# Joining the row scans of layer 1 in a two-layer scanning convolution: two scans per matmul, blocks of rows moved by quarters

## The chip, the core and the metric

One of the eight cores of a Trainium2 chip runs the whole kernel. The metric is device time in microseconds; the time before is 4159.55 us, the median of three runs (4158.39 to 4170.3). TensorE is called PE (its weight loads PEld), VectorE DVE, ScalarE ACT, GpSimd POOL and SyncE SP. SP computes nothing here: it issues transfers.

## The reference

The input x has 32 images of 48 channels, 64 rows and 128 columns, all float32. Each of two layers normalises its input (group norm, 16 groups), runs four scans over it and adds the result to the input. A scan is a recurrence: each line is the input's line plus a one-dimensional convolution (48 channels to 48, five taps along the line) of the line before it.

```python
def step(w, b):
    def f(carry, inp):
        nxt = inp + _conv1d(carry, w, b)
        return (nxt, nxt)
    return f
xs = jnp.moveaxis(x, 2, 0)                                  # rows first
d0 = xs[0]
_, d_rest = jax.lax.scan(step(down_w, down_b), d0, xs[1:])  # down, 63 steps
...
_, u_rest = jax.lax.scan(step(down_w, down_b), u0, seq)     # up, 63 steps, over the rows of D
...                                                         # right and left: 127 steps each over columns
x = x + _L0_conv_ref(_gn(x), ...)
x = x + _L1_conv_ref(_gn(x), ...)
```

The upward scan uses the weights of the downward one.

## The kernel before

The images go in four groups of eight (`GB`). A row of a group is 48 channels x 128 positions x 8 images. Eight neighbouring positions and their channels are put on the partitions (8 x 48 = 384 = `NG` = 3 groups of 128 partitions), and 16 positions x 8 images make `N` = 128 columns. A step of a scan (`step`) is then nine products (`PRODUCTS`): matmuls of a 128 x 128 block of the banded weights with 128 columns of the last line, summed in three PSUM tiles; two of the nine shift by one position and have 120 columns (112 in the column scans). Each product is executed as two instructions, so a step is 18. As soon as a sum is complete, DVE adds it, the bias and the input's line, and writes the new line in place. The nine products are ordered so that the next step starts on sums that are done first.

The work is a list of phases (`PHASES`). A rows phase handles one group of one layer: 63 steps down, then 63 steps up (`scans`, `row_step`). A cols phase handles a pair of groups: 127 steps right, 127 left. Every scan must wait for its own last step, so PE works through them one after another, in the order of the list.

SBUF holds three slots of 32 rows of a group. Phase k keeps rows 0 to 31 and 32 to 63 in the slots that `slots(k)` names; its middle slot is shared with the phase behind it. `row_views` and `row` find a row there. Normalising is done after loading: `scale_rows` on ACT, 24 instructions for a block of rows (each of 3 partition groups by 8 images).

Everything beside the scans stands on an agenda: `at(t, fn, ...)` puts a job before scan step t (a unit is one step), and `catch_up` writes the jobs into the program when the step is reached. So each engine's order, SP's too, is fixed by these numbers, and SP carries out its transfers in that order: one that must wait holds all behind it. `plan_rows` plans loads (`move_rows` in layer 0, `take_rows` in layer 1, which reads layer 0's result), scaling, and the stores of the upward scan's rows by blocks of 8 (`E8`) to the DRAM tensors `upa` and `upb` of the two layers. `plan_cols` plans the loads of the column phases from these, the residual sums and the results (`mid` for layer 0). A position's block of 16 x 8 columns divides into four quarters of 32 (`NQ`, `RUN`), one for each stage of the column scans.

`plan_input` prepares inputs 1 to 3 (groups counted from 0; they are the second to fourth): a piece of four rows per partition is loaded from `in_x` by `take_in` into one buffer `nat`, permuted by POOL (`permute`), stored to `xin` (`put_out`) and summed by ACT for the statistics (`take_others`); six pieces make a group, and `scaling` makes the factors from the sums. `pair_scaling` does so for a pair of groups of layer 1.

The names of the step tiles tell layer, group and direction: `step_12u` is layer 1, group 2, up; `step_10l` is layer 1, pair 0, left.

Of the kernel before, what the change touches and what calls it, by code (L numbers as in the profile page):

```python
# [41 lines left out]
GB = 8  # L42
E8 = 8
# [34 lines left out]
def weight_runs():  # L78
# [40 lines left out]
@with_exitstack  # L119
def kernel(  # L120
# [604 lines left out]
    def row_views(k):  # L725
        return [slot[i].rearrange("p (o h n) -> p o h n", o=NG, h=HALF) for i in slots(k)]

    def row(k, h):
        return row_views(k)[h // HALF][:, :, h % HALF]

    def move_rows(k, h0, h1, to_dram, q=None):

        _, layer, g = PHASES[k]
        view = row_views(k)[h0 // HALF]
        t = (ups if to_dram else source)[layer][g]
        for h in range(h0, h1, E8):
            end = min(h1, h + E8)
            for o in range(NG):
                for e, c0, c1, p0 in pieces(o):
                    here = view[p0 : p0 + c1 - c0, o, h % HALF : h % HALF + end - h]  # L740
# [12 lines left out]

    def take_rows(k, h0, h1, o):

        _, layer, g = PHASES[k]
        view = row_views(k)[h0 // HALF]
        for e, c0, c1, p0 in pieces(o):
            here = view[p0 : p0 + c1 - c0, o, h0 % HALF : h0 % HALF + h1 - h0]
            for q in range(NQ):  # L760
                dma(
                    here[:, :, q * RUN : (q + 1) * RUN],
                    by_quarter(source[layer][g], e, h0, h1, q)[c0:c1],
                )

    def scale_rows(k, h0, h1, groups=range(NG)):
        _, layer, g = PHASES[k]
        scale, offset = coeffs[layer, g]
        view = row_views(k)[h0 // HALF][:, :, h0 % HALF : h0 % HALF + h1 - h0]
        view = view.rearrange("p o h (k b) -> p o b h k", b=GB)  # L770
        for o in groups:
            for b in range(GB):
                args = view[:, o, b], scale[:, o, b : b + 1], offset[:, o, b : b + 1]
                nc.scalar.activation(  # L774
                    args[0], args[0], AF.Identity, bias=args[2], scale=args[1]
                )

    def scale_at_once(k, h0, h1, eng, o0=0, o1=NG):

        _, layer, g = PHASES[k]  # L780
        view = row_views(k)[h0 // HALF][:, o0:o1, h0 % HALF : h0 % HALF + h1 - h0]
        view = view.rearrange("p o h (k b) -> p o (h k) b", b=GB)
        for t, op in zip(coeffs[layer, g], (ALU.mult, ALU.add)):
            t = t[:, o0:o1].unsqueeze(2).to_broadcast([FULL, o1 - o0, (h1 - h0) * NK, GB])
            eng.tensor_tensor(view, view, t, op)
# [131 lines left out]

    def step(key, weights, b_at, src, inp, dst, whole, part):


        ps = [
            ps_step.tile([FULL, N], F32, tag=f"step{o}", name=f"step{o}_{key}")
            for o in range(NG)
        ]
        left = [sum(1 for p in PRODUCTS if p[1] == o) for o in range(NG)]
        seen = [0] * NG
        for i, o, s in PRODUCTS:
            seen[o] += 1
            m = COLUMNS.get((i, o, s), FULL)
            at = FULL * (o - NG * s - i + 1)  # L930
            nc.tensor.matmul(  # L931
                part(whole(ps[o])[0:m], -s),
                weights[:, i, at : at + m],
                part(src(i), s),
                start=seen[o] == 1,
                stop=seen[o] == left[o],
            )
            if seen[o] == left[o]:
                layer, way = b_at
                nc.vector.scalar_tensor_tensor(  # L940
                    dst(o),
                    whole(ps[o]),
                    bd[:, o, layer, way : way + 1],
                    inp(o),
                    ALU.add,
                    ALU.add,
                )

    def row_step(k, h, prev, inp, name):
        _, layer, g = PHASES[k]  # L950

        def part(t, s):
# [8 lines left out]
            lambda o: row(k, h)[:, o],  # L961
            lambda ps: ps,
            part,
        )

    def col_step(k, way, v0, v1):
# [10 lines left out]
        def part(t, s):  # L977
# [9 lines left out]
            col(v1),  # L987
            lambda ps: ps.rearrange("p (m b) -> p m b", b=GB),
            part,
        )  # L990

    def scans(k):
        if PHASES[k][0] == "rows":
            for h in range(1, H):
                yield lambda h=h: row_step(k, h, row(k, h - 1), row(k, h), "d")
            end = last.rearrange("p (o n) -> p o n", o=NG)
            for h in range(H - 2, -1, -1):
                yield lambda h=h: row_step(
                    k, h, row(k, h + 1), row(k, h - 1) if h else end, "u"
                )  # L1000
        else:
            for v in range(1, W):
                yield lambda v=v: col_step(k, RIGHT, v - 1, v)
            for v in range(W - 2, -1, -1):
                yield lambda v=v: col_step(k, LEFT, v + 1, v)

# [16 lines left out]
    def plan_input(g, times, work, lag, nats, perms):  # L1023
# [5 lines left out]
        for j, t in enumerate(times):  # L1029
            nat = nats[j % ahead]  # L1030
            if j == 0 and g > 1:
                at(t - 7, take_in, g, 0, nat)
            for i in range(per):
                perm, r = perms[i % len(perms)], i * rows // per
                at(t + i * work / per, permute, nat, r, perm, [nc.gpsimd])
                at(t + i * work / per + 4, put_out, g, rows * j + r, perm)
            at(t + lag, stats.take_others, pieces_of * j, nat)
            if j + ahead < len(times):
                free = t + 7
                at(free, take_in, g, rows * (j + ahead), nat)  # L1040
        spread(t + work + lag + (0, 2, 32, 5)[g], scaling(f"x{g}", 0, g, stats, (0, 0, 8, 0)[g]), 1)

    def plan_rows(k, t0, prev):
        if k == 1:
            ahead, scaled = (-34, -18, -3, 12), (-12, -2, 17, 33)
        elif prev == "cols":
            ahead, scaled = (-28, -12, 4, 20), (-13, 3, 19, 35)
        else:
            ahead, scaled = (-54, -43, 0, 11), (-22, -8, 16, 30)
        if k:  # L1050
            for i in range(4):
# [11 lines left out]
        if seam:  # L1063
            cuts = cuts[2:]
            end = t0 + 2 * (H - 1)
            at(end - E8, move_rows, k, E8, 2 * E8, True, 0)
# [5 lines left out]
        for h0, h1 in zip(cuts, cuts[1:]):  # L1072
            t = t0 + 2 * (H - 1) - h0
            if k == 0:
                t += 16 if h0 >= HALF else 68
            elif not following:
                t = t0 + 92 + 5 * (H - h1) / E8 + (34 if h1 <= HALF else 0)
            at(t, move_rows, k, h0, h1, True)
        at(
            t0 + H - 1,  # L1080
            nc.gpsimd.tensor_copy,
# [9 lines left out]
    def plan_cols(k, t0, prev):  # L1091
# [5 lines left out]
        for i in range(n):  # L1097
# [92 lines left out]

    starts = [0]
    for kind, *_ in PHASES:
        starts.append(starts[-1] + 2 * ((H if kind == "rows" else W) - 1))
    for k, (kind, layer, _) in enumerate(PHASES):
# [221 lines left out]
    for k in range(len(PHASES)):  # L1416
        for one in scans(k):
            catch_up(done)
            in_order(one)
            done += 1  # L1420
    catch_up(float("inf"))
# [53 lines left out]
```

## Time and profile before

| | |
|---|---|
| time, median of three runs | 4159.55 us |
| time of the profiled execution | 4158.07 us |
| its span | 4156.0 us |
| mean granted clock of TensorE | 0.989 |
| PE busy, PEld busy | 97%, 97% |
| DVE, ACT, POOL busy | 51%, 30%, 20% |
| mean DMA share, bytes | 0.79, 681 MB |
| of these by SP's queue (q1) | 582 MB, 2064256 packets |

The scans lie one behind another from 61.2 us (first step) to 4099.6 us; the last 56 us are the last results. Busy shares are of the span; a PE that is busy is not PE at its peak, since a matmul's end is modelled. Issuing a transfer is not counted as busy time of any engine, so SP's load is read from its queue's own rows (SPq), whose length is the time that the issue took.

### The profile page before, as it was taken

The page shows a single profiled execution, that of the slowest core. Times are in us where ns is not written, and L with a number is a line of the kernel's source. Part 1 is how long each engine was busy: PE and PEld are TensorE (multiplying, and loading weights), DVE is VectorE, ACT ScalarE, POOL GpSimd, SP SyncE. Part 2 cuts the span into 40 slices and gives each one's busy share as a digit, 9 for nine tenths or more (in the row PEclk, how much of TensorE's full clock was granted, in tenths as well). Part 3 has the DMA queues.
Part 4 walks back from the last instruction along what each step waited for, and adds up shares of the span by engine and source line. Part 5 has one row for each costly group of instructions (what it writes and reads, how often), then busy time and mean ns, then how long its engine had stood idle before and what let it go on. Part 6 is the DMA issues. An engine that isn't in the chain of part 4 may idle for free. (4 is left out here: it accounts for less than half of the span.)

```text
span 4156.0 us, 90019 instructions
## 1 busy us (share of the span) xinstructions
PE 4037.8 (97%) x36628; PEld 4019.1 (97%) x36628; DVE 2139.9 (51%) x6496; ACT 1251.1 (30%) x2438; POOL 832.0 (20%) x745
## 2 busy tenths in 40 slices
PE   6999989999999999999999999999999999999994
PEld 5999989999999999999999999999999999999994
DVE  6454444456654454444447665444444444444444
ACT  4645000526974553000007863423000002200122
POOL 5630010424331010010013220000000015610354
PEclk9999999999999999999999999999999999999997
DMA  9887769669979989258519979869289029999799
GB/s 299 221 187 117 126 125 209 211 146 263 206 198 166 165 170 154 44 99 189 116 26 270 183 145 149 141 98 150 49 139 208 1 56 240 301 247 157 152 235 196
DMA packets 2208798, 681.09 MB, mean 164 GB/s; under 512 B 2008976, under 2 KB 2157696, under 8 KB 2183808
## 3 DMA queue, kind: packets, MB, share of 16 engines
q1 hardware_dynamic: 2064256, 582.38, 68.9%
q10 hardware_dynamic: 141568, 87.46, 8.7%
q0 software_dynamic: 2560, 5.51, 0.5%
q8 instruction: 288, 4.72, 0.5%
q14 instruction: 126, 1.03, 0.1%
HBM read 398.32 MB, written 295.14 MB: 167 GB/s over the span
## 5 line engine op out<-in xcount | busy, mean ns | idle before, releaser
L866 POOL TENSOR_TENSOR arena<-arena 128x2048 f32<-128x2048 f32 x80 | 362.8, 4549 | 1479.8 <-PE step_10l L931 466.1
L774 ACT ACTIVATE arena<-arena,offsetr,scaler 128x256 f32<-128x256 f32 x384 | 289.3, 844 | 272.2 <-DMA arena<-mid 220.7
L711 POOL COPY arena<-arena 128x256 f32<-128x256 f32 x340 | 200.8, 651 | 482.2 <-DMA arena<-in_x 453.6
L774 ACT ACTIVATE arena<-arena,offset,scale 128x256 f32<-128x256 f32 (+2 forms) x360 | 249.0, 789 | 148.8 <-DMA arena<-xin 100.7
L931 PE MATMUL step_00r<-arena,early 128*128 128x128 f32 x2286 | 253.3, 274 | 10.5 <-DMA arena<-arena 7.1
L931 PEld LDWEIGHTS step_00r<-arena,early 128*128 128x128 f32 x2286 | 252.4, 186 | 11.4 <-issue 6.1
L650 ACT ACTIVATE early<-arena 128x256 f32<-128x256 f32 x192 | 129.6, 675 | 444.3 <-DMA arena<-xin 308.4
L931 PE MATMUL step_01r<-arena,early 128*128 128x128 f32 x2286 | 251.3, 273 | 7.6 <-DMA arena<-arena 6.2
L931 PEld LDWEIGHTS step_01r<-arena,early 128*128 128x128 f32 x2286 | 250.8, 185 | 8.1 <-issue 6.5
L931 PE MATMUL step_11r<-arena,early 128*128 128x128 f32 x2286 | 249.3, 272 | 0.3 <-DVE arena L940 0.3
L931 PEld LDWEIGHTS step_11r<-arena,early 128*128 128x128 f32 x2286 | 248.7, 184 | 0.8 <-DVE arena L940 0.7
L931 PE MATMUL step_00l<-arena,wleft 128*128 128x128 f32 x2286 | 249.0, 272 | 0.0
L931 PE MATMUL step_10r<-arena,early 128*128 128x128 f32 x2286 | 248.7, 272 | 0.0
L931 PEld LDWEIGHTS step_10r<-arena,early 128*128 128x128 f32 x2286 | 248.5, 184 | 0.2 <-DVE arena L940 0.2
L931 PEld LDWEIGHTS step_00l<-arena,wleft 128*128 128x128 f32 x2286 | 248.6, 184 | 0.0
L931 PE MATMUL step_10l<-arena,wleft 128*128 128x128 f32 x2286 | 248.5, 272 | 0.0
L931 PE MATMUL step_11l<-arena,wleft 128*128 128x128 f32 x2286 | 248.5, 272 | 0.0
L931 PEld LDWEIGHTS step_10l<-arena,wleft 128*128 128x128 f32 x2286 | 248.4, 184 | 0.0
L931 PE MATMUL step_01l<-arena,wleft 128*128 128x128 f32 x2286 | 248.4, 272 | 0.0
L931 PEld LDWEIGHTS step_11l<-arena,wleft 128*128 128x128 f32 x2286 | 248.4, 184 | 0.0
L931 PEld LDWEIGHTS step_01l<-arena,wleft 128*128 128x128 f32 x2286 | 248.4, 184 | 0.0
L298 ACT COPY early<-arena 128x1 f32<-128x1 f32 x2 | 0.4, 192 | 711.3 <-DVE arena L940 711.3
(199 smaller groups left out, 7158.0 us busy)
## 6 DMA issues: line engine op xcount, KB each, us to landing
xin<-arena SPq DMA_DIRECT2D x94, 512.0 KB, 4.1
arena<-in_x SPq DMA_DIRECT2D x18, 2048.0 KB, 11.0
arena<-xin SPq DMA_DIRECT2D x96, 384.0 KB, 9.9
arena<-mid SPq DMA_DIRECT2D x384, 96.0 KB, 3.1
upb<-arena SPq DMA_DIRECT2D x192, 192.0 KB, 3.9
arena<-upb SPq DMA_DIRECT2D x96, 384.0 KB, 12.6
arena<-xin SPq DMA_DIRECT2D x174, 192.0 KB, 4.4
mid<-arena SPq DMA_DIRECT2D x32, 1024.0 KB, 11.2
```

The source lines that it names most:

```text
L298: fn(*args)
L650: nc.scalar.activation(junk[:, 0:n], view[:, b], AF.Identity, accum_out=self.sum[:, i, j : j + 1])
L711: copy(dst[:, r, q], src[:, r0 + r, q])
L774: nc.scalar.activation(args[0], args[0], AF.Identity, bias=args[2], scale=args[1])
L866: eng.tensor_tensor(unit, unit, nat, ALU.add)
L931: nc.tensor.matmul(part(whole(ps[o])[0:m], -s), weights[:, i, at : at + m], part(src(i), s), start=seen[o] == 1, stop=seen[o] == left[o],)
```

## The change

The list of phases is reordered: layer 1's four rows phases now lie behind all of layer 0, one after another. The upward scan of group 1 runs together with the downward scan of group 2, and that of group 2 with the downward scan of group 3 (`JOINED`, `two_row_step`): each product takes 256 columns, 128 of either scan, with the columns of both scans interleaved by position (16 x 2 x 8), and DVE adds both lines in one instruction. Steps of the joint scans count two units on the agenda. Since the new group's rows come in while the old group's go out from the other end, the blocks of eight rows lie in turned order in some slots (`place`, `rows_at`). In the joint phases loads go by blocks of 8 rows, 40 transfers each, and stores too, by quarters, so that also a store of a block is 40 transfers. A load is planned 34 units ahead of its first step, the scaling 17 units ahead.

Inputs 2 and 3 are prepared over two phases each, since the rows phase of layer 1 that lay between layer 0's last two rows phases is gone from there; the loads of rows phase (0, 3) and some other jobs move on the agenda.

```diff
 PHASES:
-    ("rows", 1, 0),
     ("rows", 0, 3),
     ("cols", 0, 1),
+    ("rows", 1, 0),
     ("rows", 1, 1),
     ("rows", 1, 2),
     ("rows", 1, 3),
...
+JOINED = (8, 9)
...
+    def place(k, h):
+        first = k
+        while first in JOINED:
+            first -= 1
+        since = k - first
+        turned = (since + 1) // 2 % 2 if h < HALF else since % 2
+        c = h % HALF // E8
+        return HALF // E8 - 1 - c if turned else c
...
 def step(...):
-            ps_step.tile([FULL, N], F32, tag=f"step{o}", name=f"step{o}_{key}")
+            ps_step.tile([FULL, 2 * N], F32, tag=f"step{o}", name=f"step{o}_{key}")
...
-                part(whole(ps[o])[0:m], -s),
+                part(turn(whole(ps[o]))[0:m], -s),
                 weights[:, i, at : at + m],
-                part(src(i), s),
+                part(turn(src(i)), s),
...
+    def beside(a, b):
+        shift = b.offset - a.offset
+        assert a.ap == b.ap and shift > 0
+        return bass.AP(a.tensor, a.offset, [a.ap[0], (shift, 2), *a.ap[1:]])
...
+    def two_row_step(ku, hu, kd, hd):
...
+            lambda i: both(row(ku, hu + 1), row(kd, hd - 1), i),
+            inp,
+            lambda o: both(row(ku, hu), row(kd, hd), o),
+            lambda ps: ps.rearrange("p (c m b) -> p c m b", c=2, b=GB),
+            part,
+            lambda t: t.rearrange("p c m b -> p m c b"),
...
 def scans(k):
+                if k + 1 in JOINED:
+                    yield 2, lambda h=h: two_row_step(k, h, k + 1, H - 1 - h)
...
 def plan_input(...):
-            if j == 0 and g > 1:
-                at(t - 7, take_in, g, 0, nat)
+            if g > 1:
+                at(t - 7, take_in, g, rows * j, nat)
...
-        spread(t + work + lag + (0, 2, 32, 5)[g], scaling(f"x{g}", 0, g, stats, (0, 0, 8, 0)[g]), 1)
+        t += work + lag + (0, 2, 2, 1)[g]
+        spread(t, scaling(f"x{g}", 0, g, stats, (0, 0, 4, 0)[g]), 1)
...
 def plan_rows(k, t0, prev):
+        down, up = (2 if k in JOINED else 1), (2 if k + 1 in JOINED else 1)
+        t_up = t0 + down * (H - 1)
...
+            if not PHASES[k][1]:
+                ahead, scaled = (-33, -22, 0, 11), (-16, -5, 16, 30)
-        if k:
+        if k in JOINED:
+            for i in range(H // E8):
+                h, t = i * E8, t0 + 2 * i * E8
+                for o in range(NG):
+                    at(t - 34 + 2 * o, take_rows, k, h, h + E8, o)
+                at(t - 17, scale_rows, k, h, h + E8)
+        elif k:
...
-            t = t0 + 2 * (H - 1) - h0
+            t = t_up + up * (H - 1 - h0)
...
+            elif up == 2:
+                t += 1
...
-            at(t, move_rows, k, h0, h1, True)
+            for q in range(NQ) if up == 2 else (None,):
+                at(t, move_rows, k, h0, h1, True, q)
...
 plan_cols:
-                early = 30 if after else 46 if k == 2 else 70
+                early = 30 if after else 46 if k == 2 else 58 if k - 1 in JOINED else 70
-            spread(units[-1][0] + 14, pair_scaling(pair, stats, 3 if pair else 8), 1)
+            spread(units[-1][0] + (14 if pair else 70), pair_scaling(pair, stats, 8), 1)
...
-    times = [starts[2] + 60 + 13.5 * j for j in range(6)]
+    times = [starts[1] + 28 + 16 * j for j in range(2)]
+    times += [starts[2] + 60 + 13 * j for j in range(4)]
     plan_input(2, times, 6, 6, nats, tiles[2:4])
-    times = [t + 15 * j for t in (starts[3] + 42, starts[4] + 24) for j in range(3)]
-    plan_input(3, times, 6, 7, nats, tiles[2:4])
+    times = [starts[2] + 116 + 13 * j for j in range(2)]
+    times += [starts[3] + 42 + 13 * j for j in range(4)]
+    plan_input(3, times, 6, 6, nats, tiles[2:4])
...
-    at(starts[7] + 50, more_weights, "right", 1, RIGHT)
-    at(starts[7] + 54, more_weights, "left", 1, LEFT)
+    at(starts[6] + 50, more_weights, "right", 1, RIGHT)
+    at(starts[6] + 54, more_weights, "left", 1, LEFT)
```

PE's order, one step of the downward scan of layer 1's group 2 before (the tile's number tells which of the three sums a product goes to; the last part is the shape of the output):

```order
L931 MATMUL step_12d_23767<-arena,early 128x128
L931 MATMUL step_12d_23769<-arena,early 128x128
L931 MATMUL step_12d_23769<-arena,early 96x120
L931 MATMUL step_12d_23767<-arena,early 96x120
L931 MATMUL step_12d_23767<-arena,early 128x128
L931 MATMUL step_12d_23769<-arena,early 128x128
L931 MATMUL step_12d_23768<-arena,early 128x128
L931 MATMUL step_12d_23768<-arena,early 112x128
L931 MATMUL step_12d_23768<-arena,early 128x128
```

And the first joint step of group 1 up (row 62) and group 2 down (row 1):

```order
L954 MATMUL step_11u62d_22798<-arena,early 128x16x2x8
L954 MATMUL step_11u62d_22800<-arena,early 128x16x2x8
L954 MATMUL step_11u62d_22800<-arena,early 96x15x2x8
L954 MATMUL step_11u62d_22798<-arena,early 96x15x2x8
L954 MATMUL step_11u62d_22798<-arena,early 128x16x2x8
L954 MATMUL step_11u62d_22800<-arena,early 128x16x2x8
L954 MATMUL step_11u62d_22799<-arena,early 128x16x2x8
L954 MATMUL step_11u62d_22799<-arena,early 112x16x2x8
L954 MATMUL step_11u62d_22799<-arena,early 128x16x2x8
```

The nine products stand in the same order, each over twice the columns, and one joint step replaces two such groups of nine.

SP's order where group 1's rows of layer 1 go out (`upb_93`) and group 2's come in (`mid_86`), before: the end of 80 loads and the first stores of 40.

```order
L287 DMA arena<-mid_86 48x16x32 x8
L287 DMA arena<-mid_86 16x16x32 x4
L287 DMA arena<-mid_86 48x16x32 x8
L287 DMA arena<-mid_86 32x16x32 x4
L287 DMA upb_93<-arena 48x32x32 x2
L287 DMA upb_93<-arena 32x32x32
L287 DMA upb_93<-arena 16x32x32
L287 DMA upb_93<-arena 48x32x32 x2
```

The same place now:

```order
L288 DMA upb_93<-arena 48x8x32 x2
L288 DMA upb_93<-arena 16x8x32
L288 DMA upb_93<-arena 48x8x32 x2
L288 DMA upb_93<-arena 32x8x32
L288 DMA arena<-mid_86 16x8x32 x4
L288 DMA arena<-mid_86 48x8x32 x8
L288 DMA arena<-mid_86 16x8x32 x4
L288 DMA arena<-mid_86 48x8x32 x8
L288 DMA arena<-mid_86 32x8x32 x4
L288 DMA arena<-mid_86 48x8x32 x8
L288 DMA arena<-mid_86 32x8x32 x4
L288 DMA upb_93<-arena 48x8x32 x2
```

Loads have 8 rows of 32 columns instead of 16, stores 8 rows of one quarter instead of 32 runs (8 rows by four quarters), and 40 of the one alternate with 40 of the other. From the first store of group 1 to the last load of group 3 SP's queue has 1028 transfers.

SP's order in the third rows phase of layer 0, where input 3 is prepared (`xin_83`), before:

```order
L287 DMA xin_83<-arena 128x4x256 x4
L287 DMA arena<-in_x 128x8x512
L287 DMA arena<-mid_84 48x16x32 x8
L287 DMA arena<-mid_84 32x16x32 x4
L287 DMA arena<-mid_84 16x16x32 x4
```

And now:

```order
L288 DMA xin_83<-arena 128x4x256 x2
L288 DMA arena<-in_x 128x8x512
L288 DMA xin_83<-arena 128x4x256 x4
L288 DMA arena<-in_x 128x8x512
L288 DMA xin_83<-arena 128x4x256 x6
L288 DMA upa_90<-arena 48x32x32 x2
```

The loads of layer 1's group 0 (`mid_84`) are gone from here, and the last two pieces of input 3 follow each other in this phase instead of in the one after the next scan.

More of the change, by code (lines that the diff above doesn't have):

```diff
@@ L737, in move_rows @@
             end = min(h1, h + E8)
+            view = rows_at(k, h, end)
             for o in range(NG):
                 for e, c0, c1, p0 in pieces(o):
-                    here = view[p0 : p0 + c1 - c0, o, h % HALF : h % HALF + end - h]
+                    here = view[p0 : p0 + c1 - c0, o]
                     if to_dram:
@@ L756, in take_rows @@
         _, layer, g = PHASES[k]
-        view = row_views(k)[h0 // HALF]
+        turned = h1 - h0 > E8 and place(k, h0) > place(k, h0 + E8)
+        if turned:
+            for h in range(h0, h1, E8):
+                take_rows(k, h, h + E8, o)
+            return
+        view = rows_at(k, h0, h1)
         for e, c0, c1, p0 in pieces(o):
-            here = view[p0 : p0 + c1 - c0, o, h0 % HALF : h0 % HALF + h1 - h0]
+            here = view[p0 : p0 + c1 - c0, o]
             for q in range(NQ):
@@ L915, in let_result, with step @@
                 dma(in_output(j, half, e)[c0 * NH : c1 * NH], src[at : at + (c1 - c0) * NH])
-    def step(key, weights, b_at, src, inp, dst, whole, part):
+    def step(key, weights, b_at, src, inp, dst, whole, part, turn=lambda t: t):
         ps = [
-            ps_step.tile([FULL, N], F32, tag=f"step{o}", name=f"step{o}_{key}")
+            ps_step.tile([FULL, 2 * N], F32, tag=f"step{o}", name=f"step{o}_{key}")
             for o in range(NG)
@@ L939, in step @@
                 layer, way = b_at
[L940 to L947, printed above, removed]
+                to, sums, term = dst(o), whole(ps[o]), inp(o)
+                todo = [(to, sums, term)]
+                if isinstance(term, tuple):
+                    todo = [(to[:, c], sums[:, c], term[c]) for c in range(len(term))]
+                for to, sums, term in todo:
+                    nc.vector.scalar_tensor_tensor(
+                        to, sums, bd[:, o, layer, way : way + 1], term, ALU.add, ALU.add
+                    )
     def row_step(k, h, prev, inp, name):
@@ L961, in row_step, with lines, both, inp @@
             lambda o: row(k, h)[:, o],
-            lambda ps: ps,
+            lambda ps: ps[:, 0:N],
             part,
+        )
+    def beside(a, b):
+        shift = b.offset - a.offset
+        assert a.ap == b.ap and shift > 0
+        return bass.AP(a.tensor, a.offset, [a.ap[0], (shift, 2), *a.ap[1:]])
+    def lines(t):
+        return t.rearrange("p (m b) -> p m b", b=GB)
+    def two_row_step(ku, hu, kd, hd):
+        _, layer, g = PHASES[ku]
+        first = slots(ku)[0] < slots(kd)[0]
+        def both(u, d, o):
+            u, d = lines(u[:, o]), lines(d[:, o])
+            return beside(*((u, d) if first else (d, u)))
+        def inp(o):
+            if hu:
+                return both(row(ku, hu - 1), row(kd, hd), o)
+            pair = lines(last.rearrange("p (o n) -> p o n", o=NG)[:, o]), lines(row(kd, hd)[:, o])
+            return pair if first else pair[::-1]
+        def part(t, s):
+            return t[:, max(0, s) : NK + min(0, s)]
+        step(
+            f"{layer}{g}u{hu}d{hd}",
+            wt[f"down{layer}"],
+            (layer, DOWN),
+            lambda i: both(row(ku, hu + 1), row(kd, hd - 1), i),
[4 more added lines that the diff above has]
+            lambda t: t.rearrange("p c m b -> p m c b"),
         )
@@ L993, in scans @@
         if PHASES[k][0] == "rows":
-            for h in range(1, H):
-                yield lambda h=h: row_step(k, h, row(k, h - 1), row(k, h), "d")
+            if k not in JOINED:
+                for h in range(1, H):
+                    yield 1, lambda h=h: row_step(k, h, row(k, h - 1), row(k, h), "d")
             end = last.rearrange("p (o n) -> p o n", o=NG)
             for h in range(H - 2, -1, -1):
-                yield lambda h=h: row_step(
-                    k, h, row(k, h + 1), row(k, h - 1) if h else end, "u"
-                )
+                if k + 1 in JOINED:
+                    yield 2, lambda h=h: two_row_step(k, h, k + 1, H - 1 - h)
+                else:
+                    yield 1, lambda h=h: row_step(
+                        k, h, row(k, h + 1), row(k, h - 1) if h else end, "u"
+                    )
         else:
             for v in range(1, W):
-                yield lambda v=v: col_step(k, RIGHT, v - 1, v)
+                yield 1, lambda v=v: col_step(k, RIGHT, v - 1, v)
             for v in range(W - 2, -1, -1):
-                yield lambda v=v: col_step(k, LEFT, v + 1, v)
+                yield 1, lambda v=v: col_step(k, LEFT, v + 1, v)
     agenda = []
@@ L1064, in plan_rows @@
             cuts = cuts[2:]
-            end = t0 + 2 * (H - 1)
+            end = t_up + up * (H - 1)
             at(end - E8, move_rows, k, E8, 2 * E8, True, 0)
@@ L1188, in last_results @@
             store_result(k, 0, i, perm)
-    starts = [0]
-    for kind, *_ in PHASES:
-        starts.append(starts[-1] + 2 * ((H if kind == "rows" else W) - 1))
+    starts, end = [], 0
+    for k, (kind, *_) in enumerate(PHASES):
+        n = (H if kind == "rows" else W) - 1
+        starts.append(end - 2 * n if k in JOINED else end)
+        end = starts[-1] + (2 if k in JOINED else 1) * n + (2 if k + 1 in JOINED else 1) * n
     for k, (kind, layer, _) in enumerate(PHASES):
@@ L1416 @@
     for k in range(len(PHASES)):
-        for one in scans(k):
+        for units, one in scans(k):
             catch_up(done)
             in_order(one)
-            done += 1
+            done += units
     catch_up(float("inf"))
```

24 lines of the change are left out of this document (13 added, 11 removed).

## The prediction

> **What bounds the kernel now.** I read the page first, then the windows by stage, the list of who waited for whom on PE, and last the queue of SP, which issues nearly all transfers.
>
> ```profile
> span 4156.0 us, 90019 instructions
> PE 4037.8 (97%) x36628; PEld 4019.1 (97%) x36628; DVE 2139.9 (51%) x6496; ACT 1251.1 (30%) x2438; POOL 832.0 (20%) x745
> ...
> 2605.00:2730.70 125.70, 125.47 (x1138) 124.97 (x1137) 60.91 (x190) 63.18 (x84) 0.00 (x0) 1.00 0.86 136
> 2730.70:2855.00 124.30, 124.30 (x1135) 124.30 (x1135) 60.37 (x189) 37.21 (x50) 0.50 (x1) 1.00 0.68 109
> 2855.00:2980.00 125.00, 125.00 (x1134) 124.55 (x1134) 60.66 (x190) 2.50 (x4) 0.00 (x0) 1.00 0.54 96
> ```
>
> The last three rows are group 2 of layer 1 down, the same group up, and group 3 down (columns: window, length, PE, PEld, DVE, ACT, POOL busy, granted clock, DMA share, GB/s). PE is busy for all of each window at full clock. Here TensorE is the only bound, and everything else has slack. PE's waits in the whole run are few, and all lie at the start or at the seams from rows to columns:
>
> ```profile
> PE rows L1333 <- POOL arena L711: 19.9, 1, 19.9
> PE step_00d L931 <- DVE arena L785: 9.2, 1, 9.2
> PE step_00r L931 <- DMA arena<-arena: 7.1, 2, 5.8
> PE step_01r L931 <- DMA arena<-arena: 6.2, 1, 6.2
> L931 PE MATMUL step_12u<-arena,early x1134: 266/275/282, 2730.7 to 2855.0; 128*128 128x128 f32 x126, 128*96 128x120 f32 x63
> ```
>
> The last row gives the price of one step of a row scan: 63 steps of 18 instructions from 2730.7 to 2855.0 are 124.4 us with the last instruction, so 1.975 us a step and 0.110 us an instruction.
>
> SP's queue in the same stage (start, length, name, count):
>
> ```profile
> 2497.12 50.52 SPq L287 DMA_DIRECT2D arena<-mid  x80
> 2547.74 39.18 SPq L287 DMA_DIRECT2D upb<-arena  x40
> 2587.01 49.22 SPq L287 DMA_DIRECT2D arena<-mid  x80
> 2636.33 41.10 SPq L287 DMA_DIRECT2D upb<-arena  x40
> 2677.52 48.47 SPq L287 DMA_DIRECT2D arena<-mid  x80
> 2744.29 56.41 SPq L287 DMA_DIRECT2D upb<-arena  x40
> ```
>
> A group's 64 rows come in by 160 loads and go out by 80 stores. SP issues back to back for nearly 230 us from 2497 to 2726. So one group already costs SP about 98 us of loads (48.5 to 50.5 for 80) and 80 us of stores, 178 of the 250 us that its scans last. SP is second in line, and the page's table of engines does not show it.
>
> **The joint scans on PE.** Each of the 126 pairs of steps becomes one step of 18 instructions with 256 columns (240 for the shifted ones). The nearest longer matmul:
>
> ```profile
> 27.83 11.32 PE L1333 MATMUL rows<-arena,wleft 128*128 128x512 f32 x26
> L1333 PE MATMUL rows<-arena,wleft x40: 592/592/1219, 19.9 to 38.6; 128*128 128x512 f32 x40
> ```
>
> 26 of them take 11.32 us, the last lasting 0.592: (11.32 - 0.592) / 25 = 0.429 us for 512 columns, 0.215 for 256. Two single instructions are 0.220. Between these I take 0.216 and, for 240 columns, 0.2025: 14 x 0.216 + 4 x 0.2025 = 3.83 us a joint step against 3.95. That is 0.12 x 126 = 15 us if nothing else holds PE; the ends are 0 (no gain a column) and 18. No row shows a read that jumps between two rows every 8 elements. The nearest are the column scans, which read in pieces of 8 too:
>
> ```profile
> L931 PE MATMUL step_10l<-arena,wleft x2286: 259/275/328, 3353.5 to 3601.7; 128*128 128x128 f32 x128, 128*96 128x112 f32 x63
> L940 DVE SCALAR_TENSOR_TENSOR arena<-step_02d,bd,arena x189: 281/351/353, 1087.5 to 1218.3; 128x128 f32<-128x128 f32 x189
> ```
>
> 248.3 us for 2286 instructions are 0.109 each, no more than in the row scans, so I add nothing. A sum on DVE takes 0.351 us now and at most 0.70 for twice the columns; between a sum and the matmul that reads it stand four products, 8 x 0.216 = 1.7 us, so it stays covered.
>
> **The joint scans on SP.** This term decides. Blocks of 8 rows are now loaded by 40 transfers (before: 16 rows by 40) and stored by 40 (before: 10), since each of ten pieces is cut into four quarters. For groups 2 and 3 in, and 1 and 2 out, that is 640 loads and 640 stores instead of 320 and 160. The same small store exists already, at the seam after group 1 of a pair:
>
> ```profile
> 1908.73 18.01 SPq L287 DMA_DIRECT2D upa<-arena  x33
> L287 SPq DMA_DIRECT2D upa<-arena x33: 428/470/1610, 1908.7 to 1926.3; - x33
> DMA to landing us min/median/max: 1.6/1.8/3.9
> upa<-arena SPq DMA_DIRECT2D x84, 48.0 KB, 2.1
> arena<-mid SPq DMA_DIRECT2D x384, 96.0 KB, 3.1
> ```
>
> 33 of them back to back take 18.01 us, 0.546 each, and 0.512 without the one of 1.61 us. They land in 1.8 us, and by the program's semaphores each waits only for the one issued eight earlier (4 us ago), so landing does not hold them: issuing does. A load of double size costs 48.47 / 80 = 0.606. So halving a transfer's bytes hardly makes its issue cheaper, and I price both small kinds at 0.53, with 0.51 and 0.58 (stores 0.546, loads still 0.606) as ends. Forty cost 21.2 us, a block in and a block out 42.4; the scan needs such a pair every 8 joint steps, 30.6 us. SP falls behind by about 12 us per block.
>
> How far follows from SP's order, shown with the change. Count time from the first joint step. The store of group 1's last block waits for joint step 8, at 31 us. From there SP has no pause: 1028 transfers, blocks out and blocks in by turns, up to the last load of group 3. They end at 31 + 1028 x 0.53 = 576 us. The last third then lands (2.4 us) and is scaled:
>
> ```profile
> L774 ACT ACTIVATE arena<-arena,offset,scale 128x128 f32<-128x128 f32 x40 | 20.7, 610 | 19.8 <-DMA arena<-xin 19.8
> ```
>
> 8 x 20.7 / 40 = 4.1 us. So joint step 56 of the second pair can go on at 582 us. Before, the same rows were reached after 2 x (63 + 55.7) single steps, 469 us. The difference, **113 us**, is stall net of the 15 us that the joint matmuls save: whatever PE saves here only waits longer. The loads have a lead of 34 units (a unit is one step of a single scan), which lasts up to the sixth block of the first pair: its loads end 31 + (5 x 40 + 28) x 0.53 = 152 us, and with 6 us more it misses joint step 40, at 153 us. From there on PE stands at the start of each block, eleven times, 113 + 15 = 128 us in all, or 11 to 12 us each. What is late next: only 8 joint steps, then group 3's upward scan of 124 us, in which SP's 120 remaining stores (64 us) and the first column loads fit. Anything else that slows PE between two such waits only shortens the next one.
>
> [...]
>
> **Inputs 3 and 4 over two phases each.** Input 4 must now be ready one phase earlier: four of its six pieces go through one buffer during the third row phase. Its cycle:
>
> ```profile
> 1179.11 1.27 SPq L287 DMA_DIRECT2D arena<-in_x  x1
> 1212.74 0.37 SPq L287 DMA_DIRECT2D arena<-in_x  x1
> 1238.24 1.26 SPq L287 DMA_DIRECT2D arena<-in_x  x1
> DMA to landing us min/median/max: 8.6/11.0/13.7
> L582 ACT ACTIVATE early<-arena 128x512 f32<-128x512 f32 x144 | 90.8, 631 | 267.7 <-DMA arena<-in_x 263.6
> L574 ACT ACTIVATE early<-arena,neg_x_x 128x512 f32<-128x512 f32 x144 | 104.0, 722 | 4.7
> L574 ACT ACTIVATION_READ_ACCUMULATOR early<-arena,neg_x_x 128x1 f32 x144 | 26.9, 187 | 0.0
> L931 PE MATMUL step_02u<-arena,early x1134: 266/275/377, 1218.1 to 1345.2; 128*128 128x128 f32 x126, 128*96 128x120 f32 x63
> 1480.40 19.75 SPq L287 DMA_DIRECT2D arena<-xin  x19
> 324.00:448.50 124.50, 124.50 (x1137) 124.50 (x1136) 60.63 (x190) 44.66 (x60) 2.36 (x3) 1.00 0.69 106
> ```
>
> The first three pieces' loads are issued 34 and 26 us apart (the line below them is their time to landing). The fourth would be issued near 1264, land 11 us later, and be summed by ACT in 8 x (0.631 + 0.722) + 16 x 0.187, 13.8 us, until about 1289. DVE's part of the scaling stands in its order near step 95 of that phase, the 32nd of the upward scan, at 1218 + 32 x 2.0 = 1282, and DVE works in order: a stall of 0 to 9 us, I take 4. The first 16 rows of the next phase load right behind it (20 us for 20 transfers), in time for its start at 1345. Two pieces of input 3 move into the row phase of the last line, where POOL, which permutes them, is busy for 2 of 124 us. The relaxed pair scaling and the moved weight loads have their cover on POOL and ACT unchanged: nothing.
>
> Against the profiled execution's own 4158.1 (1.5 below the median of 4159.6, to which I predict): 4159.6 + 113 + 4 = **4277 us**.
>
> **Rivals.** *SP keeps up.* An SP issue that stands alone takes less:
>
> ```profile
> L287 SPq DMA_DIRECT2D arena<-upa x120: 302/308/2300, 487.0 to 1998.5; - x120
> ```
>
> At about 0.35 the 1028 end at 391 us, well before 463, nothing stalls, and the 15 us are gained: 4159.6 - 15 + 4 = 4149, faster. It decides below 0.42 a transfer. Against it stand the 33 in a row at 428 or more; for it, only lone issues. Chance 0.09. [...] *Issue is dearer*: the joint stage mixes loads and stores on the 16 DMA engines, as the load rows do at 0.606; 1028 x 0.61 = 627 gives +195 and 4359. Against it, halved bytes; 0.10. *The main case*, 0.76.
>
> **Range and chances.** The main case by its ends 0.51 and 0.58 reaches from 4256 to 4328, and with 0 to 9 us for input 4 and a queue that starts up to 10 us late, 4240 to 4345. I give 4215 to 4345, which leaves out the fast rival and most of the dear one. 0.3% (12 us) is what a measurement here tells from no change: faster 0.09, same 0.05, slower 0.86.
>
> **What would show it.** Right: in the joint stage SP's rows without gaps, about 0.53 us apiece, 40 and 40 in turn; PE and DVE waiting for ACT's scaling or for the loads from mid at every eighth joint step, 8 to 13 us each; joint matmuls 0.216 us apart; the joint stage 90 to 130 us longer than the same 252 single steps were. Wrong: SP rows near 0.4 us with pauses at the stores' waits (then the kernel is faster), or PE stalls elsewhere, above all in the third row phase (input 4) or a joint matmul far above 0.216.

## The result: 2.7% slower, and the profile after

The changed kernel takes 4272.27 us (median of six runs, 4268.5 to 4281.04), the kernel before 4158.87 us (median of six, 4146.94 to 4170.3). The ratio is 1.0273, 95% interval 1.0256 to 1.029. The profiled execution took 4269.46 us, with a span of 4267.5 against 4156.0 before. The head of its page:

```profile
span 4267.5 us, 86313 instructions
PE 4048.6 (95%) x34360; PEld 3950.1 (93%) x34360; DVE 2073.5 (49%) x6124; ACT 1306.7 (31%) x2630; POOL 823.0 (19%) x745
```

2268 matmuls fewer (126 x 18), and yet PE is busy 11 us longer than the 4037.8 before, with 95% of the span instead of 97%.

The windows over the joint stage, of the kernel before (its 252 single steps) and of the kernel after (the 126 joint steps, then the same split at the first stall). Columns: window, length, PE, PEld, DVE, ACT and POOL busy, granted clock, DMA share, GB/s.

```profile
2478.00:2980.40 502.40, 502.17 (x4562) 500.61 (x4561) 248.57 (x794) 149.38 (x205) 4.77 (x14) 1.00 0.73 119
```

```profile
2496.10:2680.20 184.10, 184.10 (x867) 157.87 (x866) 66.79 (x143) 54.62 (x105) 0.50 (x1) 1.00 0.46 73
2680.20:3092.00 411.80, 327.50 (x1404) 273.01 (x1404) 110.21 (x240) 119.81 (x231) 0.51 (x1) 0.87 0.48 77
2496.10:3092.00 595.90, 511.60 (x2270) 430.88 (x2269) 177.00 (x383) 174.44 (x335) 1.01 (x2) 0.91 0.48 76
```

The stage grew from 502.4 to 595.9 us, by 93.5. Its first 48 joint steps run without a gap, 184.1 / 48 = 3.835 us each. The other 78 would need 299.2 us at that pace and took 411.8. Of the 112.6 us lost, 84.3 are idle (411.8 - 327.5), and the remaining 28.3 are matmuls that ran longer: the granted clock is 0.87 over this window. The DMA share *fell*, from 0.73 to 0.48, so the DMA engines are not what is short.

Who waited for whom on PE, after (in total, times, longest):

```profile
PE step_00r L954 <- DMA arena<-arena: 21.8, 1, 21.8
...
PE step_12u62d L954 <- DMA arena<-mid: 11.1, 1, 11.1
PE step_11u14d L954 <- DMA arena<-mid: 9.8, 1, 9.8
...
PE step_12u6d L954 <- DMA upb<-arena: 7.5, 1, 7.5
```

Ten stalls of 7 to 11 us, at the joint steps u14 and u6 of the first pair and u62, u54 and so on to u6 of the second: at the start of each block of 8 rows, from the seventh block on. The step with the stall also runs slower. The second pair's u6, with its stall inside, and the step after it (durations in ns: least, median, most):

```profile
L954 PE MATMUL step_12u6d<-arena,early x18: 379/607/793, 3054.9 to 3068.9; 128*128 128x256 f32 x12, 128*96 128x240 f32 x4, 128*112 128x256 f32 x2
L954 PE MATMUL step_12u5d<-arena,early x18: 366/379/379, 3069.1 to 3072.7; 128*128 128x256 f32 x12, 128*96 128x240 f32 x4, 128*112 128x256 f32 x2
```

One more stall was not there before: 21.8 us at the first column seam, where the kernel before waited 7.1 in two for the same transfers.

SP's queue in the joint stage, the first and last rows of 26 (start, length, name, count):

```profile
2521.96 20.81 SPq L288 DMA_DIRECT2D upb<-arena  x40
2542.81 20.29 SPq L288 DMA_DIRECT2D arena<-mid  x40
2563.20 21.02 SPq L288 DMA_DIRECT2D upb<-arena  x40
2584.27 21.49 SPq L288 DMA_DIRECT2D arena<-mid  x40
...
3021.59 21.03 SPq L288 DMA_DIRECT2D upb<-arena  x40
3042.66 13.96 SPq L288 DMA_DIRECT2D arena<-mid  x28
```

Each row begins where the one above it ends. From 2521.96 to 3056.62 SP issues 1028 transfers, 534.7 us, 0.520 each: 41.6 us for a block out and a block in, where eight joint steps take 30.7.

### The profile page after: what moved, and what is told of

It reads as the page before. It is cut to its first block, busy times and chain, and to the rows that moved or that the text cites. A ratio compares the mean times of both kernels' runs of the same rounds, so it can differ in the third digit from the quotient of the medians.

```text
span 4267.5 us, 86313 instructions
## 1 busy us (share of the span) xinstructions
PE 4048.6 (95%) x34360; PEld 3950.1 (93%) x34360; DVE 2073.5 (49%) x6124; ACT 1306.7 (31%) x2630; POOL 823.0 (19%) x745
## 5 line engine op out<-in xcount | busy, mean ns | idle before, releaser
L797 ACT ACTIVATE arena<-arena,offsetr,scaler 128x128 f32<-128x128 f32 (+1 forms) x576 | 344.4, 685 | 490.6 <-DMA arena<-mid 447.6
L954 PE MATMUL step_00r<-arena,early 128*128 128x128 f32 x2286 | 251.4, 273 | 23.7 <-DMA arena<-arena 21.8
L911 ACT COPY arena<-arena 128x256 f32<-128x256 f32 x172 | 99.7, 655 | 364.3 <-POOL arena L889 245.9
## 6 DMA issues: line engine op xcount, KB each, us to landing
arena<-upb SPq DMA_DIRECT2D x96, 384.0 KB, 11.3
arena<-mid ACTq DMA_DIRECT2D x29, 1024.0 KB, 11.3
```

The lines of the kernel that those rows point to most:

```text
L797: nc.scalar.activation(args[0], args[0], AF.Identity, bias=args[2], scale=args[1])
L911: copy(by_w(perm)[:, a], src[:, a])
L954: nc.tensor.matmul(part(turn(whole(ps[o]))[0:m], -s), weights[:, i, at : at + m], part(turn(src(i)), s), start=seen[o] == 1, stop=seen[o] ...
```

## The experiments

Two theories stood against each other for the joint stage: SP's issue time per transfer, or something that goes with the transfers themselves (bytes, the DMA engines, a load that must wait for the store of its place). For the seam: SP late because of the third input's two pieces (group 2, "input 3" in the expectations), or the DMA engines late. Each edit is against the changed kernel if nothing else is said. Times are medians, followed by the ratio to the kernel before, run beside it, and that ratio's 95% interval.

**Fewer stores.**

```diff
-            for q in range(NQ) if up == 2 else (None,):
+            for q in (None,):
```

> The joint scans as changed, but each block of 8 rows is stored by 10 transfers instead of 40. If SP's issue time is the bound: from the first waiting store on, 140 stores of about 1.0 us and 468 loads of 0.52 are 386 us, less than the 463 us that the steps need, so SP gets pauses, the ten stalls go, the joint stage lasts 126 x 3.84 = 484 us instead of 596, and the time is about 4160 us (4155 to 4175). If the bound is the chain in each place (block out, block in, scaling) or the loads: stalls stay, 4230 us or more.

Measured: 4266.54 us, 1.026 (1.0243 to 1.0277), joint stage 591.4 us. The stalls stayed, but they are other stalls: sixteen, nearly all of 4 to 6 us, two or three steps into a block, and SP now has pauses. Two of PE's, and then DVE's wait between 2500 and 2700 us:

```profile
PE step_11u37d L954 <- DVE arena L968: 6.4, 1, 6.4
PE step_11u29d L954 <- DVE arena L968: 6.3, 1, 6.3
```

```profile
DVE arena L968 <- DMA upb<-arena: 26.0, 4, 7.5
```

PE waits for a sum, and DVE, before it writes that sum (joint step u54, rows 54 of one group and 9 of the other), waits for the store of rows 56 to 63 to land. It touches none of them. By the program's addresses its write is one operation over two rows 12,928 elements apart, and for the two of the three sums that wait, a stored block lies in between. So this run missed its forecast and did not test SP; it showed another wait, which the quarters avoid.

**The same stores from another queue.**

```diff
-                at(t, move_rows, k, h0, h1, True, q)
+                at(t, move_rows, k, h0, h1, True, q, nc.gpsimd if up == 2 else None)
```

> Stores by quarters as changed, the same 640 transfers and bytes, but issued on POOL's queue instead of SP's. SP's issue time as the bound: SP has only 21 us of loads per 30.7 us of steps, so the joint stage falls from 596 to about 484 to 495 us and the time to 4160 to 4172 us. If small transfers as such, the DMA engines, or the wait of a load for the store of its place set the pace: the stage stays near 596 us and the time near 4270.

Measured: 4157.39 us, 0.9995 (0.9986 to 1.0004). The joint stage:

```profile
2497.80:2980.60 482.80, 482.80 (x2271) 414.49 (x2270) 177.42 (x383) 175.52 (x336) 358.34 (x602) 1.00 0.49 97
```

The stores on POOL, a group of the page (busy, mean ns of one, idle before):

```profile
L288 POOL DMA_DIRECT2D upb<-arena x640 | 381.2, 604 | 109.7 <-DVE arena L968 107.3
```

PE is busy for all of the 482.8 us, at full clock. The same 640 stores with the same bytes cost POOL 0.604 us apiece, more than SP's 0.520, but beside SP's loads instead of between them. The 113 us by which the stage fell (595.9 to 482.8) were time that transfers stood in line on one queue. It was not the wait of a load for the store of its place either: in this run SP waits 160.7 us in all (from 2490 to 2980 us of its trace) for stores to land, and PE still stands for none. The DMA share hardly moved, 0.48 in the changed kernel and 0.49 here: issues of 0.520 us, one behind another on one queue, were the joint stage's whole loss.

**Whole stores, sums row by row.** The first run's edit, and:

```diff
+                elif len(to.shape) == 4:
+                    todo = [(to[:, c], sums[:, c], term[:, c]) for c in range(2)]
```

> Blocks stored whole on SP (10 transfers), and each joint sum on DVE written as two operations, one for each row, instead of one over both rows. The run with whole stores alone had DVE waiting 26 us in 200 us for stores of a block that it does not touch. If that wait belongs to the two-row write (the program takes the whole stretch between the two rows as written): the 16 stalls of about 5 us go, SP has pauses, the joint stage is 484 to 492 us, time 4160 to 4170 us. If whole stores are slow for another reason (SP, landing of bigger stores): the stage stays near 591 us and the time near 4266.

Measured: 4158.28 us, 1.0006 (0.9983 to 1.0029).

```profile
2496.40:2979.20 482.80, 482.80 (x2270) 414.25 (x2269) 219.50 (x755) 175.80 (x336) 1.01 (x2) 1.00 0.59 95
```

The wait of DVE belongs to the two-row write together with whole stores: with either undone it goes. Here SP does everything, 10 stores and 40 loads per block, and PE never waits. Twice as many sums cost DVE 42 us (219.5 against 177.4) and PE nothing. Why a store by quarters is not taken as overlapping was not followed.

**More loads.** SP relieved of the stores as above, and each load of the joint stage cut in two:

```diff
+            step = E8 // 2 if k in JOINED else h1 - h0
             for q in range(NQ):
-                dma(... h0, h1 ...)
+                for h in range(h0, h1, step):
+                    dma(... h, h + step ...)
```

> Stores on POOL's queue, and SP's loads of the joint stage cut in two: 80 transfers of half the bytes for a block of 8 rows, 1280 in all. Bytes and arithmetic are the same. If SP's issue per transfer is the bound: 80 x 0.49 = 39 us per block against 30.7 us of steps, the stalls come back, the joint stage grows from 483 to 600 to 640 us and the time to 4275 to 4315 us. If bytes or the number of stores count: 483 us, 4157.

Measured: 4295.52 us, 1.0324 (1.03 to 1.0349). The joint stage, and SP's queue:

```profile
2500.50:3126.50 626.00, 519.46 (x2270) 434.81 (x2269) 176.90 (x383) 187.75 (x360) 358.38 (x602) 0.91 0.40 77
```

```profile
2489.11 601.67 SPq L288 DMA_DIRECT2D arena<-mid  x1200
```

0.501 us each, back to back, with the DMA share down to 0.40. The same bytes as in the run with POOL's stores, the same stores, 138 us more: the number of issues on one queue decides, for these at 0.501 us as for stores and loads by turns at 0.520.

**Quarters without joint scans.** The kernel before, with groups 1 and 2 of layer 1 stored by quarters:

```diff
-            at(t, move_rows, k, h0, h1, True)
+            for q in range(NQ) if k in (7, 8) else (None,):
+                at(t, move_rows, k, h0, h1, True, q)
```

> The kernel before (single scans), with groups 1 and 2 of layer 1 stored by quarters. SP's issue as the bound: 160 loads x 0.606 + 320 stores x 0.52 = 263 us per group against 250 us of scans, so SP falls 13 us behind per group, most of it within its lead: 4160 to 4185 us. If quarters cost by bytes or packets, or nothing: 4160. So near the bound, quarters alone are nearly free: the loss needs the loads in blocks of 8 rows as well.

Measured: 4181.74 us, 1.0045 (1.003 to 1.0061). Within the range, but "nearly free" was wrong:

```profile
2500.96 48.97 SPq L287 DMA_DIRECT2D arena<-mid  x80
2550.03 88.13 SPq L287 DMA_DIRECT2D upb<-arena  x160
2638.25 47.57 SPq L287 DMA_DIRECT2D arena<-mid  x80
2685.92 87.12 SPq L287 DMA_DIRECT2D upb<-arena  x160
```

```profile
PE step_13d L931 <- DMA arena<-mid: 15.2, 1, 15.2
```

The stores cost 0.55 us, so a group costs SP 272 us (2500.96 to 2773.14) against some 250 of scans. The backlog of two groups comes out at the last group's downward scan, which takes 147.1 us instead of 125.3.

**Order and inputs alone.**

```diff
-JOINED = (8, 9)
+JOINED = ()
```

> The new order of phases and the inputs over two phases, without joint scans and without quarters. The traces put 11 us of the loss at the seam to the first column phase and some 5 us elsewhere ahead of the joint stage: 4170 to 4176 us, the seam stalling 20 to 24 us as in the changed kernel. The prediction's steps gave 4 us for this part: 4163, with a stall in the third row phase. If the stall at the seam hangs on the joint part: 4159.

Measured: 4171.98 us, 1.0039 (1.0025 to 1.0054), with a stall of 21.8 us at the first column seam as in the changed kernel. So the seam's loss hangs on the new order and the inputs, not on the joint scans.

**The third input's two pieces on other queues.** SP's queue before and after, ahead of the seam, is what to explain (`arena<-arena` are the seam's rows):

```profile
423.86 13.80 SPq L287 DMA_DIRECT2D wleft<-taps  x25
...
562.59 32.52 SPq L287 DMA_DIRECT2D arena<-arena  x47
```

```profile
393.56 7.42 SPq L288 DMA_DIRECT2D xin<-arena  x4
404.09 0.37 SPq L288 DMA_DIRECT2D arena<-in_x  x1
...
458.38 13.00 SPq L288 DMA_DIRECT2D wleft<-taps  x25
...
580.47 32.00 SPq L288 DMA_DIRECT2D arena<-arena  x47
```

SP is 34 us late at the column weights and 18 at the seam. First, the pieces on ACT's queue:

```diff
+            queue = nc.scalar if g == 2 and j < 2 else None
-                at(t - 7, take_in, g, rows * j, nat)
+                at(t - 7, take_in, g, rows * j, nat, queue)
...
-                at(t + i * work / per + 4, put_out, g, rows * j + r, perm)
+                at(t + i * work / per + 4, put_out, g, rows * j + r, perm, queue)
```

> As changed, but the two pieces of input 3 that were moved into the second row phase are loaded and put out on ACT's queue instead of SP's. If SP is late at the seam because it stands behind these pieces' waits for POOL: SP reaches the seam's rows near 562 us instead of 580, the stall of 21.8 us falls to 6 to 10, time about 4260 us (11 less). If the order of phases or the DMA load makes the seam late: 4272, no change.

Measured: 4274.68 us, 1.0282 (1.0265 to 1.0299), stall 21.2 us: no gain. But SP still waited for these transfers to land, though it no longer issued them; why was not followed:

```profile
SPq L288 <- DMA xin<-arena: 23.4, 4, 12.8
SPq L288 <- DMA arena<-in_x: 5.4, 1, 5.4
```

Then on POOL's queue (`nc.gpsimd` in the same place, and POOL's stores in the joint stage):

> The quarters' stores on POOL's queue, and besides the two pieces of input 3 in the second row phase loaded and put out on POOL's queue. On ACT's queue these pieces still held SP, which waited 23 us for their landing. If SP's lateness at the seam comes from these pieces on its own queue or on ACT's: the stall at the first column seam falls from 22 to 6 to 10 us, 4157 less 11, about 4146 us, faster than before by 0.3%. If the DMA engines are what is late there (their share is 0.9 to 1.0 from 470 to 580 us): the stall stays at 20 to 22 us, 4157.

Measured: 4163.48 us, 1.0001 (0.999 to 1.0012), stall 25.1 us. One wait was left on SP:

```profile
SPq L288 <- POOL early L340: 23.9, 1, 23.9
```

POOL clears the buffer of the column weights (a memset of about 1 us) in its own order, behind the second piece's copies. And on its own queue POOL issues that piece's load only when ACT has summed the first piece, for which it stood 144.4 us:

```profile
412.82 0.90 POOL L288 DMA_DIRECT2D arena<-in_x  x1 [144.43 <-ACT early L575]
421.50 9.47 POOL L712 COPY arena<-arena 128x256 f32<-128x256 f32 x16 [7.38 <-DMA arena<-in_x]
432.51 1.08 POOL L340 MEMSET early<- 128x1152 f32 x1
```

The same with whole stores and sums row by row:

> Blocks stored whole on SP with the sums written row by row, and the two pieces of input 3 on POOL's queue. If both causes are as thought: joint stage 484 to 492 us and a stall of 6 to 10 us at the seam, 4147 to 4157 us. If only the joint part is: 4160 to 4170.

Measured: 4166.21 us, 1.001 (1.0 to 1.002), stall 25.4 us, joint stage 482.8. So the joint part came out as thought and the seam did not; the run repeats both findings.

**The weights ahead of the pieces.** Whole stores, sums row by row, and:

```diff
-    times = [starts[1] + 28 + 16 * j for j in range(2)]
+    times = [starts[1] + 34 + 16 * j for j in range(2)]
...
-    at(starts[1] + 40, spread_row_masks)
-    at(starts[1] + 50, more_weights, "right", 0, RIGHT)
-    at(starts[1] + 54, more_weights, "left", 0, LEFT)
+    at(starts[1] + 24, spread_row_masks)
+    at(starts[1] + 25, more_weights, "right", 0, RIGHT)
+    at(starts[1] + 26, more_weights, "left", 0, LEFT)
```

> As whole stores with sums row by row (joint stage 483 us), and at the seam: the masks' spread and the column weights of layer 0 are moved ahead of input 3's two pieces on POOL and SP (units 24 to 26 of the second row phase instead of 40 to 54; the pieces at 34 and 50 instead of 28 and 44). With the pieces on POOL's queue SP had waited 23.9 us for POOL's clearing of the weight buffer, which stood in POOL's order behind the pieces' copies. If that wait and the pieces' own waits made SP late: SP is at the seam's rows some 10 to 18 us earlier than at 580, the stall of 21 us falls to 6 to 14, 4146 to 4153 us. If the DMA engines are late: stall 20 us, 4158.

Measured: 4157.52 us, 0.9988 (0.9979 to 0.9996), stall 25.9 us. The weights are early now, but SP waits 15.6 us for POOL's copies, with the stores behind it, and is at the seam's rows at 583. By time and stall alone, this run and the three before it came out as the rival, late DMA engines, would have it. With the pieces on POOL's queue as well:

> The same order, with the two pieces' transfers on POOL's queue, so that SP waits for nothing of them. If SP's waits are the cause: stall at the seam 6 to 10 us, 4146 us. If the DMA engines are late: 20 us, 4158 to 4166.

Measured: 4148.54 us, 0.9961 (0.9949 to 0.9973), 0.4% faster than the kernel before. SP and PE:

```profile
566.01 31.71 SPq L288 DMA_DIRECT2D arena<-arena  x47
```

```profile
PE step_00r L954 <- DMA arena<-arena: 9.1, 1, 9.1
```

The same bytes pass through the same DMA engines, and SP is at the seam's rows at 566 instead of 583. So two waits of SP made the seam late: for POOL's copies of the pieces, and for POOL's memset, which stands in POOL's order behind them. Each alone was enough, which is why taking away one of them moved nothing. The DMA engines have a part in it as well: their share is 0.91 to 1.00 from 470 us to the seam in the changed kernel, which leaves SP little room to make up for lost time; but from 440 to 470 us, when SP is late, it is 0.52, and in this last run 1.01.

## Why the prediction was right, and where it was not

The direction, the place and the mechanism came out as forecast. That 4272.27 lies only 5 us from the 4277 is partly luck: the joint stage cost 19.5 us less than its term, and 18 us came in elsewhere, where the prediction had 4.

- *Joint step.* Forecast 3.83 us, measured 3.835; the sums on DVE stayed covered (PE is busy for all of the 184.1 us of the first 48 steps). The gain was put at 15 us. With SP out of the way the stage takes 482.8 instead of 502.4, so 19.6: the stretch before lasted 4.7 us more than 252 steps of 1.975. That is not all gain. The 4562 matmuls of that stretch are 26 more than 252 x 18, and 24 of them are the small ones of pair 1's scaling, which PE ran in group 1's upward scan (127.2 us instead of 124.5). The new order puts them into an earlier phase.
- *SP decides.* Right, shown from both sides: stores off its queue end the stalls (482.8 us), more loads on it bring them back (626.0 us) at a DMA share of 0.40.
- *The price and the 113 us.* Measured 93.5. 1028 x (0.53 - 0.520) = 10 us less, the queue began 25.9 us after the first joint step instead of 31, 5 less (the first store needs seven joint steps and not eight, since row 63 has no upward step), and 4.7 from the row above. The term of 6 us for landing and scaling held: the last load was issued 560.5 us into the stage, and 93.5 + 469 + 4.7 = 567 is when the step could go on.
- *Eleven stalls of 11 to 12 us from the sixth block on.* Ten, from the seventh, 112.6 / 10 = 11.3 us each: 8.4 idle and 2.8 of slower matmuls behind it. The prediction did not split these two. The stalls are 7 to 11 us long, the mean granted clock is 0.87 over their stretch and 1.00 over the 48 joint steps ahead of it, and u6's slowest matmul takes 0.793 us where the next step's take 0.379; why the clock falls there was not shown.
- *The fourth input, 4 us near step 95 of the third row phase.* Not there: in that upward scan, where it was put, PE waits 0.3 us, and the scan takes 127.5 us against 127.2 before. Zero was the low end of its range. The prediction's list of PE's waits left out 5.0 us within the downward scan of this phase (step_02d, put down to "issue"), which are 7.3 now.
- *"Two pieces of input 3 ... nothing."* Wrong, and the one step of reasoning that failed. Both row scans of the phase keep their pace, but from the start of its upward scan to the end of the first column phase it takes 648.5 us instead of 637.5 (from the first matmul of the scans in the traces), 11.0 more. The prediction looked at POOL's free time alone. The pieces' transfers stand in SP's order, SP waits there 14.4 us for POOL's copies with 20 stores and 60 weight loads behind it, and POOL's memset for those weights waits behind the copies.
- *What is left.* 111.5 us of span are 93.5 of the joint stage, 11.0 of the seam and 7 in shifts of up to 2 us in other phases. In two of these (03d and 10u, 1.5 and 1.3 us longer) PE now runs small matmuls of the scaling; the rest was not followed.

The rivals: SP at 0.35 fell by the rows without gaps at 0.520, the dearer issue of 0.61 by the same rows. The issue price in mixed order was below both 0.53 and the 0.606 of the double-size loads. The chance of 0.05 for no change would take a price of about 0.42 (31 + 1028 x 0.42 + 6 = 469); no run shows that for stores and loads by turns, and the cheapest of the joint stage's 26 rows has 0.499 (13.96 / 28). Single issues can be shorter: the prediction's row of lone ones has 0.302 at the least, and so have the joint stage's shortest.

The whole change thus has two costs that its idea does not need. The new order of phases is needed, by the program's order of work: in the old one the scaling that makes group 2's factors runs during group 1's upward scan, too late for joint rows, the first of which must be scaled before that scan begins. No run tested that. The quarters are needed only while one operation writes two rows.

## What to carry over

Count the transfers of a stage per queue and multiply by the back-to-back price before the stage is made shorter: here a queue that issued without pauses (1028 transfers at 0.520 us) was a bound like an engine, though no table of engines shows it, and the DMA share fell while it bound, from 0.73 to 0.48. When a job moves to an idle engine, follow every order it enters (its loads and stores on their queue, and what that engine must do next for somebody else), since free time of the engine says nothing of those who stand behind its waits: POOL was busy for 2 of 124 us where the pieces went, and SP then waited 14.4 us for its copies. And where an experiment leaves the time unchanged, see first whether the same wait is still there: here another wait had taken its place more than once.

## What was not expected of the hardware and the program

- SP's price follows the size only weakly: 0.520 us over loads and stores of the joint stage, 0.501 for loads of half the bytes, 0.606 for loads of twice and 0.98 for stores of four times the bytes in the kernel before; 0.55 for stores by quarters in the single scans. POOL's queue took 0.604 for the stores, and ran beside SP without slowing it (its loads have a median of 0.441 us there, 0.470 in the changed kernel) or PE.
- Moving a transfer to ACT's queue did not free SP: it waited 23.4 us for the landing of stores that ACT had issued.
- A write over two far rows in one operation waited up to 7.5 us for a store of rows that lie between them.
